# Values of a windowed attention: one projection and a trip through DRAM in place of four products on repeated tokens

## The chip, the cores and the metric

The kernel runs on one core of a Trainium2 chip. The core has TensorE (PE: matrix products into PSUM, with PEld for its weight loads), VectorE (DVE), ScalarE (ACT), GpSimd (POOL) and SyncE (SP), which here only issues DMAs. Each engine works through its own queue in order. PSUM has eight banks of 128 partitions by 512 float32. The metric is the device time of one execution in microseconds (us), median of the runs; smaller is better.

## The reference

Two transformer blocks with adaptive layernorm over x of 4 batches x 1024 tokens x 128 features, all float32. Block 0 is a linear attention and a mixture of 16 experts. Block 1 is a windowed attention with 16 heads of 8 features, then a feed-forward part that itself holds two local-attention layers ("block 1's second attention"). The change touches block 1's first attention alone:

```
h = layernorm(x) * (1 + ca) + sa
q, k, v = split(h @ w_qkv.T), 16 heads of 8
scores: causal, the last 64 tokens (key position >= 16), and the first 16 tokens as a global prefix
out = softmax(scores) @ v, heads joined, @ w_out.T
x = x + ga * out
```

## The kernel before

Activations lie with the features on the partitions and the tokens along the free dimension: `hT[b]` is 128 features x 1024 tokens of batch b. Block 1's first attention goes through 32 tiles of 128 tokens: four batches `b`, eight tiles `t` each. A tile has four chunks `c` of 32 tokens, and the 16 heads are handled as four groups of four.

For the sum of probabilities times values, 32 keys of a chunk and the four heads of a group share the 128 partitions of one product: partition 32h + k is key k for head h of the group. So V is needed in a form in which each partition block h holds the same 32 tokens, with everything but the features of head h set to zero. That is the tile `vb`, 128 x (16 x 32), where the 16 are four chunks times four groups. The mask `hm32` (a part of the constant `hx`) is one where the feature belongs to the partition block's head.

`values(b, t)` (L648 to L656) makes it. GpSimd copies the tile's tokens four times side by side into `hr` (L650). For each chunk TensorE multiplies the repeated tokens with the value weights (L653), four products of 128x128x128 into one PSUM bank `vp`, so that the repetition appears on the output's partitions. VectorE multiplies the bank with the mask into `vb` (L655).

The other functions of a step, with the lines that the prediction names:

- `maxima` (transposes of `nm`, L296) and `scores` (L267, L273, L282, row maxima on VectorE L285, then `nm` L289 and L290) work ahead: the maxima of the next tile, the scores of the one after that.
- `weights` (L666, L671, L677) forms the transposed scores for two groups at a time in PSUM, and ScalarE takes the exponentials into `pt` (L680).
- `outputs` of the tile before (L706, L715) sums probabilities times `vb` and, beside it, the denominators, in one PSUM bank `o`; VectorE then takes the reciprocal (L725) and the product `os` (L726). It reads the `vb` of its own tile and, for its first two chunks, of the tile before.
- `prefix` (L692, L693) puts the scores of the 16 prefix tokens into the second half of that same bank `o`, and ScalarE takes their exponentials `pg` (L697).
- At certain tiles: `queries` (L224), `keys` (L236, copied by VectorE L238, then masked by GpSimd into `kg` and `kx`, L240 and L243), `prefix_values` (`vgp` L255), `project_out` (`y`, L731), the layernorms (`tokens`, `normed`, with three GpSimd operations L148 to L150), and `rotary`, ten GpSimd operations that prepare tables for the second attention.

The order of a step is this (L755 and on):

```
when(g + 1, maxima); when(g + 2, scores)
queries, tokens, normed at certain tiles
when(g, weights, (0, 1)); when(g - 1, outputs)
prefix_values at t == 1
when(g, weights, (2, 3)); when(g, values); when(g, prefix)
rotary, project_out, keys at certain tiles
```

TensorE's order is exactly the order in which the code issues its work. The other engines' queues and the DMA queue are ordered by a planner, which simulates the program and issues what is ready, earlier code first; a dependency or a full set of buffers becomes a wait in the queue. `rotary` is pinned behind whatever GpSimd instruction stands before it in the code. PSUM's eight banks go to the tags "s" (4), "t" (2), "o" (1) and "m" (1); the bank "m" is shared by `vp`, `vgp`, `qp`, `kp`, `y` and the layernorm transposes. `hr` has three buffers, `vb` four. Transfers in this stage are few: before it SP issues the weights of the second attention and the table `tab` (L597 to L646), and in it two pairs of `hs` transfers (L612, L615).

Of the kernel before, what the change touches and what calls it, by code (L numbers as in the profile page):

```python
# [19 lines left out]
F32 = mybir.dt.float32  # L20
BF16 = mybir.dt.bfloat16
AF = mybir.ActivationFunctionType
ALU = mybir.AluOpType
# [3 lines left out]
P = 128  # L27
B, N, D = 4, 1024, 128
# [20 lines left out]
def adaln_blocks(ctx: ExitStack, tc: tile.TileContext, a: dict, out: bass.AP):  # L49
    nc = tc.nc  # L50
    pe, act, dve, pool = nc.tensor, nc.scalar, nc.vector, nc.gpsimd
# [4 lines left out]
    def const(name, shape, dtype=F32):  # L56
        return cp.tile(shape, dtype, tag=name, name=name)
# [54 lines left out]
    with tc.tile_pool(name="modps", bufs=2, space=PSUM) as mp:  # L112
        sc = const("sc", [P, 2, B])
        act.activation(sc, cT, AF.Silu)
        for blk in range(2):
            ps = mp.tile([P, 6, B], F32, tag="mod", name=f"modps{blk}")
            for j in range(6):
                pe.matmul(ps[:, j, :], lhsT=wmod[:, blk, j * D : (j + 1) * D], rhs=sc[:, blk, :], start=True, stop=True)
            m = const(f"mod{blk}", [P, 6, B])
# [39 lines left out]
    m = mods[0]  # L159
    hT = [hp.tile([P, N], F32, tag=f"hT{b}", name=f"hT{b}") for b in range(B)]  # L160
# [18 lines left out]
    wqkv1 = const("wqkv1", [P, 3, D])  # L179
# [24 lines left out]
    KB = 32  # L204
# [3 lines left out]
    hm32, hm64 = hx[:, 0:32], hx[:, 32:96]  # L208
    ps = both.enter_context(tc.tile_pool(name="ps", bufs=1, space=PSUM))
    kept1 = {}  # L210
# [8 lines left out]
    def queries(b, k):  # L219
        s = slice(k * BLK, (k + 1) * BLK)  # L220
        if k == 0:
            kept1[b, "q"] = of(b).tile([P, N], F32, tag="q", name=f"q1_{b}")
        qp = ps.tile([P, BLK], F32, tag="m", name=f"qp_{b}_{k}")
        pe.matmul(qp, lhsT=wqkv1[:, 0, :], rhs=hT[b][:, s], start=True, stop=True)  # L224
        act.activation(kept1[b, "q"][:, s], qp, AF.Copy, scale=scale1)

    def keys(b, k):
        s = slice(k * BLK, (k + 1) * BLK)
        if k == 0:
            kept1[b, "kx"] = of(b).tile([P, NC, 4, KB], F32, tag="kx", name=f"kx_{b}")  # L230
            kept1[b, "kg"] = of(b).tile([P, H0, PREFIX], F32, tag="kg", name=f"kg_{b}")
            kept1[b, "nmt"] = of(b).tile([P, N + 2 * KB], BF16, tag="nmt", name=f"nmt_{b}")
            pool.memset(kept1[b, "nmt"][:, N:], 0.0)
        kx, kg = kept1[b, "kx"], kept1[b, "kg"]
        kp = ps.tile([P, BLK], F32, tag="m", name=f"kp_{b}_{k}")
        pe.matmul(kp, lhsT=wqkv1[:, 1, :], rhs=hT[b][:, s], start=True, stop=True)  # L236
        kt = pre.tile([P, BLK], F32, tag="k", name=f"k1_{b}_{k}", bufs=2)
        dve.tensor_copy(kt, kp)  # L238
        if k == 0:
            pool.tensor_tensor(kg, kt[:, 0:PREFIX].unsqueeze(1).to_broadcast([P, H0, PREFIX]), bc(hm16, [P, H0, PREFIX]), ALU.mult)  # L240
        for i in range(4):
            c0 = 16 * k + 4 * i
            pool.tensor_tensor(  # L243
                kx[:, c0 : c0 + 4],
                kt[:, i * P : (i + 1) * P].rearrange("p (c k) -> p c k", k=KB).unsqueeze(2).to_broadcast([P, 4, 4, KB]),
                hm4.unsqueeze(1).unsqueeze(3).to_broadcast([P, 4, 4, KB]),
                ALU.mult,
            )

    def prefix_values(b):  # L250

        hr = pre.tile([P, 8, PREFIX], F32, tag="hrg", name=f"hrg_{b}", bufs=2)
        pool.tensor_copy(hr, hT[b][:, 0:PREFIX].unsqueeze(1).to_broadcast([P, 8, PREFIX]))
        vp = ps.tile([P, D], F32, tag="m", name=f"vgp_{b}")
        pe.matmul(vp, lhsT=hr.rearrange("p h k -> p (h k)"), rhs=wqkv1[:, 2, :], start=True, stop=True)  # L255
        vg = pre.tile([P, 2, 64], F32, tag="vg", name=f"vg_{b}", bufs=2)
        dve.tensor_tensor(vg, vp.rearrange("p (g c) -> p g c", g=2), hm64.unsqueeze(1).to_broadcast([P, 2, 64]), ALU.mult)
        kept1[b, "vg"] = vg
# [360 lines left out]
    def rotary(tab, ab, l):  # L619

        here = tc.keep_in_program_order
        qk0 = R_QK + l * 2 * DH
        for w in range(2):
            for half in range(2):
                to, of = slice(32 * half, 32 * half + 32), qk0 + w * DH + 32 - 32 * half
                here(pool.tensor_tensor(
                    ab[:, 1, :, w, to], tab[:, 1, :, w, to], rows[:, of : of + 32].unsqueeze(1).to_broadcast([P, NT, 32]), ALU.mult
                ))
            of = qk0 + w * DH
            here(pool.tensor_tensor(  # L630
                ab[:, 0, :, w, :], tab[:, 0, :, w, :], rows[:, of : of + DH].unsqueeze(1).to_broadcast([P, NT, DH]), ALU.mult
            ))
        for i in range(2):
            here(pool.tensor_scalar(ab[:, i, :, 0, :], ab[:, i, :, 0, :], 8.0, None, ALU.mult))


    m = mods[1]
    with (
        tc.tile_pool(name="w6o", bufs=1) as wo6,
        tc.tile_pool(name="w6b", bufs=2) as wb,  # L640
        tc.tile_pool(name="w6", bufs=3) as wp,
        tc.manual_schedule(engines={mybir.EngineType.PE}),
# [3 lines left out]
        nc.sync.dma_start(out=tab, in_=a["tab"])  # L646
        def values(b, t):

            hr = wp.tile([P, 4, 4, KB], F32, tag="hr", name=f"hr_{b}_{t}")
            pool.tensor_copy(hr, hT[b][:, t * P : (t + 1) * P].rearrange("p (c k) -> p c k", k=KB).unsqueeze(2).to_broadcast([P, 4, 4, KB]))  # L650
            vp = ps.tile([P, 4, D], F32, tag="m", name=f"vp_{b}_{t}")
            for c in range(4):
                pe.matmul(vp[:, c, :], lhsT=hr[:, c].rearrange("p h k -> p (h k)"), rhs=wqkv1[:, 2, :], start=True, stop=True)  # L653
            v = wp.tile([P, 16, 32], F32, tag="vb", name=f"vb_{b}_{t}", bufs=4)
            dve.tensor_tensor(v, vp.rearrange("p c (j e) -> p (c j) e", e=32), hm32.unsqueeze(1).to_broadcast([P, 16, 32]), ALU.mult)  # L655
            kept1[b, t, "v"] = v  # L656

        def weights(b, t, js):
            nt = f"{b}_{t}"
# [68 lines left out]
        def project_out(b, k):  # L728
            s = slice(k * BLK, (k + 1) * BLK)
            yp = ps.tile([P, BLK], F32, tag="m", name=f"y1_{b}_{k}")  # L730
            pe.matmul(yp, lhsT=wout1, rhs=kept1[b, k, "os"], start=True, stop=True)  # L731
            dve.scalar_tensor_tensor(xT[b][:, s], yp, mods[1][:, 2, b : b + 1], xT[b][:, s], ALU.mult, ALU.add)  # L732
# [18 lines left out]
        def when(g, f, *args):  # L751
            if 0 <= g < NG8:
                f(*divmod(g, NT), *args)

        for g in range(NG8 + 2):  # L755
            b, t = divmod(g, NT)
            ahead = b + 1 < B
            when(g + 1, maxima)
            when(g + 2, scores)
            if ahead and t in (2, 4):  # L760
                queries(b + 1, t // 2 - 1)
            for after, k, f in ((6, 0, tokens), (8, 0, normed), (11, 1, tokens), (13, 1, normed)):
                if (g - after) % NT == 0 and 0 <= (g - after) // NT < B - 1:
                    f((g - after) // NT, k, "h3")
            for at, k, f in ((1, 0, tokens), (3, 0, normed), (5, 1, tokens), (7, 1, normed)):
                if g == at:
                    f(B - 1, k, "h2")
            when(g, weights, (0, 1))
            when(g - 1, outputs)
            if ahead and t == 1:  # L770
                prefix_values(b + 1)
            when(g, weights, (2, 3))
            when(g, values)
            when(g, prefix)
            if t == 5 and 0 < b <= DEPTH:
                rotary(tab, abs_[b - 1], b - 1)
            if g % 4 == 1 and g > 4:
                project_out((g - 5) // NT, (g - 5) % NT // 4)
            if ahead and t in (3, 5):
                keys(b + 1, t // 2 - 1)  # L780
# [6 lines left out]
    with (  # L787
# [214 lines left out]
        for l in range(DEPTH):  # L1002
            for b in range(B):
                g = (l * B + b) * NT
# [18 lines left out]
        for g in range(-2, tiles + 12):  # L1023
            side = steps.get(g, [])
            when(g, scores)
            when(g + 2, project, 0)
            when(g - 1, flip, 0)
            when(g + 2, project, 1)
            when(g - 1, flip, 1)
            when(g + 1, turn, 0)  # L1030
            when(g - 2, outputs, 0)
            for f, args in side[:1]:
                f(*args)
            when(g + 1, turn, 1)
            when(g - 2, outputs, 1)
            when(g, values)
            when(g - 3, back)

            f0 = g - 7 if g < tiles - 2 else g - 6
            if f0 % 4 == 0 and 0 <= f0 < tiles and g != tiles - 1:  # L1040
                project_out(f0 // (B * NT), f0 // NT % B, f0 % NT // 4)
            for f, args in side[1:]:
                f(*args)
# [148 lines left out]
```

## Time and profile before

| | |
|---|---|
| median of 3 runs | 1399.29 us (1398.83 to 1407.56) |
| profiled execution | 1399.1 us, span of its instructions 1397.3 us |
| the stage of the change, first `vp` matmul to last `os` | 342.6 to 654.3 us |
| mean granted TensorE clock | 0.982 of full speed |
| `vp` matmuls L653 | 256 records (two for each product), from 342.6 to 649.1 us |
| `hr` copies L650 on GpSimd | 32, 0.61 us each |
| masking multiplies L655 on VectorE | 32, 0.69 us each |

A row of the timeline is start, duration, engine, line, operation, output and inputs with partitions x elements, and how often. In groups of instructions the numbers are total busy time, mean time of one in ns, and the idle time before them with what ended it. The chain of waits is followed back from the last instruction, at each step to what released it; its rows are start, time on the chain, engine, tile, line. "PEclk" or "granted clock" is the TensorE clock as a share of full speed.

### The profile page before, as it was taken

The page shows a single profiled execution, that of the slowest core. Times are in us where ns is not written, and L with a number is a line of the kernel's source. Part 1 is how long each engine was busy: PE and PEld are TensorE (multiplying, and loading weights), DVE is VectorE, ACT ScalarE, POOL GpSimd, SP SyncE. Part 2 cuts the span into 40 slices and gives each one's busy share as a digit, 9 for nine tenths or more (in the row PEclk, how much of TensorE's full clock was granted, in tenths as well). Part 3 has the DMA queues.
Part 4 walks back from the last instruction along what each step waited for, and adds up shares of the span by engine and source line. Part 5 has one row for each costly group of instructions (what it writes and reads, how often), then busy time and mean ns, then how long its engine had stood idle before and what let it go on. Part 6 is the DMA issues. An engine that isn't in the chain of part 4 may idle for free.

```text
span 1397.3 us, 33849 instructions
## 1 busy us (share of the span) xinstructions
PE 1311.6 (94%) x13908; PEld 810.3 (58%) x13908; DVE 885.1 (63%) x2090; ACT 702.8 (50%) x1453; POOL 730.6 (52%) x750
## 2 busy tenths in 40 slices
PE   5799988997999999998899999999999999999997
PEld 4544544444777677676466566656666566666553
DVE  5655444523555555554788778877788777887753
ACT  2463532321222222222576776767667776677752
POOL 4454537461232405211987676666767667766620
PEclk9799999998999999999899999999999999999999
DMA  6031221213000000000111111111211111111111
GB/s 180 0 123 55 68 67 57 69 53 121 3 3 3 17 3 18 3 3 3 24 33 45 38 43 32 24 43 33 48 34 25 43 32 43 44 35 36 40 35 30
DMA packets 38655, 56.14 MB, mean 40 GB/s; under 512 B 6331, under 2 KB 18661, under 8 KB 38373
## 3 DMA queue, kind: packets, MB, share of 16 engines
q1 hardware_dynamic: 37204, 52.44, 14.1%
q8 instruction: 110, 1.80, 0.5%
q10 hardware_dynamic: 1296, 1.54, 0.3%
q14 instruction: 45, 0.36, 0.1%
HBM read 27.24 MB, written 2.36 MB: 21 GB/s over the span
## 4 chain that ended last, share of the span: by engine, by line
PE 77%; DVE 8%; POOL 7%; ACT 3%; issue 3%; DMA 1%; POOLq 0%; ACTq 0%; SPq 0%
PE qk L802 7%; PE v L844 4%; PE o L903 4%; PE s L873 4%; PE t L677 4%; PE yp L927 4%; PE qktr L829 4%; PE ptr L890 3%; PE o L715 3%; PE gm L961 3%; PE h L494 3%; PE a L970 3%; PE ym L978 3%; PE vp L653 3%; POOL u L498 2%
## 5 line engine op out<-in xcount | busy, mean ns | idle before, releaser
L819 POOL TENSOR_TENSOR co<-co,si 128x512 f32<-128x512 f32 x128 | 162.7, 1273 | 129.1 <-DVE si L812 128.7
L818 POOL TENSOR_TENSOR ss<-ss,nhalf 128x16 f32<-128x16 f32 x64 | 187.2, 2925 | 4.7
L882 ACT ACTIVATE pr<-s,mx,ss 128x128 f32<-128x128 f32 x512 | 186.5, 480 | 1.8
L805 ACT ACTIVATE sq<-qk 128x512 f32<-128x512 f32 x128 | 79.5, 621 | 171.7 <-PE qk L802 98.1
L802 PE MATMUL qk<-wqkv,hs 128*128 128x512 f32 x256 | 137.2, 620 | 0.8 <-DVE xT L732 0.8
L498 POOL TENSOR_TENSOR u<-u,cw 128x512 f32<-128x512 f32 x64 | 81.1, 1270 | 93.2 <-ACT u L497 74.5
L494 PE MATMUL h<-hT,w 128*128 128x512 f32 x256 | 122.1, 597 | 1.6 <-DVE g L500 1.6
L877 DVE TENSOR_REDUCE mx<-s 128x4 f32<-128x512 f32 x128 | 82.3, 684 | 56.1 <-PE s L873 56.0
L500 DVE TENSOR_TENSOR g<-u,h 128x512 f32<-128x512 f32 x64 | 43.7, 685 | 114.8 <-POOL u L498 112.6
L285 DVE TENSOR_REDUCE mx<-s 128x4 f32<-128x448 f32 x128 | 70.9, 616 | 70.4 <-PE s L282 70.4
L680 ACT ACTIVATE pt<-t 128x384 f32<-128x384 f32 x128 | 55.8, 488 | 116.9 <-PE t L677 116.9
L650 POOL COPY hr<-hT 128x512 f32<-128x512 f32 x32 | 19.5, 614 | 176.4 <-PE vp L653 172.3
L807 DVE TENSOR_TENSOR co<-qk,ab 128x512 f32<-128x512 f32 x128 | 87.7, 685 | 28.6 <-ACT sq L805 28.3
L890 PEld LDWEIGHTS ptr<-ident,pr 128*128 128x128 f32 x512 | 63.6, 141 | 64.8 <-issue 53.4
L829 PE MATMUL qktr<-ident,co 128*128 128x128 f32 x512 | 78.1, 275 | 11.5 <-POOL co L821 10.5
L497 ACT ACTIVATE u<-h 128x512 f32<-128x512 f32 x64 | 38.3, 598 | 97.3 <-PE h L494 90.4
L903 PE MATMUL o<-vs,pt 128*64 128x65 f32 x1024 | 86.9, 228 | 0.0
L812 DVE TENSOR_TENSOR si<-qk,ab 128x512 f32<-128x512 f32 x128 | 86.8, 678 | 0.0
L903 PE MATMUL o<-ve,pt 128*64 128x65 f32 x1024 | 86.6, 227 | 0.0
L814 DVE TENSOR_REDUCE ss<-sq 128x8 f32<-128x512 f32 x128 | 86.2, 673 | 0.0
L494 PEld LDWEIGHTS h<-hT,w 128*128 128x128 f32 x256 | 47.8, 192 | 61.9 <-issue 53.5
L903 PEld LDWEIGHTS o<-ve,pt 128*64 128x64 f32 x1024 | 69.2, 137 | 23.1 <-issue 16.1
(234 smaller groups left out, 3060.6 us busy)
## 6 DMA issues: line engine op xcount, KB each, us to landing
cw<-cd SPq DMA_DIRECT2D x128, 128.0 KB, 3.1
ve<-vs SPq DMA_DIRECT2D x120, 130.0 KB, 2.3
hs_m<-hT SPq DMA_DIRECT2D x24, 128.0 KB, 2.2
xin<-in_x SPq DMA_DIRECT2D x4, 512.0 KB, 6.9
hs<-hT SPq DMA_DIRECT2D x8, 256.0 KB, 2.9
out<-out SPq DMA_DIRECT2D x8, 256.0 KB, 2.5
hs<-hT SPq DMA_DIRECT2D x8, 255.8 KB, 3.7
w<-in_w SPq DMA_DIRECT2D x3, 512.0 KB, 5.0
```

Of the source, the lines that this page charges most:

```text
L494: pe.matmul(h, lhsT=w[:, c * P : (c + 1) * P], rhs=hT[b][:, blk(k)], start=True, stop=True)
L498: pool.tensor_tensor(u, u, kept[b, k, "cw"][:, c, :], ALU.mult)
L802: pe.matmul(ps, lhsT=hs[l, b][:, t * P : (t + 1) * P], rhs=wl[l][0][:, w, :], start=True, stop=True)
L807: dve.tensor_tensor(co, ph, abs_[l][:, 0, t, w, :].unsqueeze(1).to_broadcast([P, HEADS, DH]), ALU.mult)
L812: dve.tensor_tensor(si.rearrange("p h (i e) -> p h i e", i=2), ex, sn, ALU.mult)
L814: dve.tensor_reduce(ss[:, w, :], sq, AX.X, ALU.add)
L818: pool.tensor_tensor(ss, ss, nhalf[:, 0:2].unsqueeze(2).to_broadcast([P, 2, HEADS]), ALU.pow)
L819: pool.tensor_tensor(co, co, si, ALU.add)
L829: pe.transpose(tp[:, i, :], co[:, i * P : (i + 1) * P], ident)
L882: act.activation(pr[:, c, :], S[j][:, c, :], AF.Exp, bias=mx[:, j, c : c + 1], scale=rq[:, j, c : c + 1])
L890: pe.transpose(tp[:, c, :], pr[:, c, :], ident)
L903: pe.matmul(o[qs, c, :], lhsT=pt[:, c, qs], rhs=vv[:, 2 * c + j, :], start=True, stop=True)
```

## The change

V of a tile is projected once: one product of the tile's 128 tokens with the value weights, tokens on the partitions. ScalarE copies it from PSUM to `v` in SBUF. A DMA writes `v` to a DRAM tile `vd` (64 KB), and four DMAs read it back, one for each partition block h, each placing token k of chunk c at partition 32h + k: 32 partitions x 4 chunks x 128 features, 64 KB in pieces of 512 bytes. GpSimd multiplies the result `vr` with the mask into `vb`. All five DMAs are issued by SP. `hr` and the VectorE multiply are gone. `vb` has five buffers instead of four.

The values of a tile are made one step sooner: `values(0, 0)` stands before the loop, and step g makes the values of tile g + 1 at the place where it made those of tile g.

```diff
         tc.tile_pool(name="w6o", bufs=1) as wo6,
+        tc.tile_pool(name="w6d", bufs=3, space=bass.MemoryType.DRAM) as dr6,
...
         def values(b, t):
 
-            hr = wp.tile([P, 4, 4, KB], F32, tag="hr", name=f"hr_{b}_{t}")
-            pool.tensor_copy(hr, hT[b][:, t * P : (t + 1) * P].rearrange("p (c k) -> p c k", k=KB).unsqueeze(2).to_broadcast([P, 4, 4, KB]))
-            vp = ps.tile([P, 4, D], F32, tag="m", name=f"vp_{b}_{t}")
-            for c in range(4):
-                pe.matmul(vp[:, c, :], lhsT=hr[:, c].rearrange("p h k -> p (h k)"), rhs=wqkv1[:, 2, :], start=True, stop=True)
-            v = wp.tile([P, 16, 32], F32, tag="vb", name=f"vb_{b}_{t}", bufs=4)
-            dve.tensor_tensor(v, vp.rearrange("p c (j e) -> p (c j) e", e=32), hm32.unsqueeze(1).to_broadcast([P, 16, 32]), ALU.mult)
-            kept1[b, t, "v"] = v
+            vp = ps.tile([P, D], F32, tag="m", name=f"vp_{b}_{t}")
+            pe.matmul(vp, lhsT=hT[b][:, t * P : (t + 1) * P], rhs=wqkv1[:, 2, :], start=True, stop=True)
+            v = wp.tile([P, D], F32, tag="v", name=f"v_{b}_{t}", bufs=2)
+            act.copy(v, vp)
+            vd = dr6.tile([P, D], F32, tag="vd", name=f"vd_{b}_{t}")
+            nc.sync.dma_start(out=vd, in_=v)
+            vr = wp.tile([P, 4, D], F32, tag="vr", name=f"vr_{b}_{t}")
+            for h in range(4):
+                nc.sync.dma_start(out=vr[32 * h : 32 * h + 32], in_=vd.rearrange("(c k) f -> k c f", k=KB))
+            vb = wp.tile([P, 16, 32], F32, tag="vb", name=f"vb_{b}_{t}", bufs=5)
+            pool.tensor_tensor(vb, vr.rearrange("p c (j e) -> p (c j) e", e=32), hm32.unsqueeze(1).to_broadcast([P, 16, 32]), ALU.mult)
+            kept1[b, t, "v"] = vb
...
+        values(0, 0)
         for g in range(NG8 + 2):
...
             when(g, weights, (2, 3))
-            when(g, values)
+            when(g + 1, values)
             when(g, prefix)
```

## The prediction

> **What bounds the kernel now.** I read the page's busy times first, then the busy times of stretches inside the stage that the change touches (block 1's first attention, 342 to 653 us), then the chain of waits through it.
>
> ```profile
> PE 1311.6 (94%) x13908; PEld 810.3 (58%) x13908; DVE 885.1 (63%) x2090; ACT 702.8 (50%) x1453; POOL 730.6 (52%) x750
> ```
>
> The average does not decide; the stretches do (columns: length, then busy us of each engine, granted clock, DMA share, GB/s):
>
> ```profile
> core 0: us, PE busy (x) PEld busy (x) DVE busy (x) ACT busy (x) POOL busy (x), PEclk, DMA share, GB/s
> 420.00:500.00 80.00, 79.16 (x1608) 57.26 (x1592) 44.34 (x95) 22.53 (x54) 27.18 (x33) 1.00 0.04 9
> 580.00:653.00 73.00, 72.36 (x1625) 55.26 (x1622) 34.34 (x71) 20.81 (x51) 5.66 (x8) 1.00 0.01 3
> ```
>
> TensorE is busy 99% of the stage at full granted clock; VectorE 55%, GpSimd 34%, ScalarE 28%, the DMA engines near nothing. A busy TensorE need not be at its peak, so I checked in the chain of waits that the values' matmuls lie on the path:
>
> ```profile
> 433.20 0.42 PE vgp L255 x2
> ...
> 434.04 0.86 PE t L677 x16
> 434.91 1.09 PE vp L653 x8
> 436.00 0.22 PE o L692 x2
> ```
>
> From 345 to 653 the chain is TensorE alone; `vp` L653 holds 11.0% of those 308 us, 1.06 us a tile. The row above it is the twin of what the change leaves: `vgp`, one 128x128 float32 product (two records, x2), takes 0.42 us where four take 1.09.
>
> **What the change removes from the path.** A tile goes from four products to one: 1.09 - 0.42 = 0.67 us. The timeline agrees: `vp`'s eight records start 445.73, the next matmul at 446.73, 1.00 us, and six records of eight at the even pace of 0.11 us are 0.67.
> - Steps 1 to 30: 30 x 0.67 = 20.1 us.
> - Step 0: its `vp` ran at a granted clock of 0.67 (336 to 346 us) and took 1.87 us to the next matmul (342.63 to 344.50); six eighths are 1.4, I take 1.3.
> - Step 31 has no values any more: 0.9.
> - Tile 0's product now stands before the loop, behind the scores that end at 330.26. TensorE idles there from 330.3 to 333.0 for VectorE's `nm` (2.77 us): cost 0; without that gap, 0.4.
>
> Together -22.3 us.
>
> **What it adds, off the path if it is in time.** VectorE loses 32 x 0.69 us, GpSimd 32 `hr` copies of 0.61. ScalarE gains 32 copies 128x128 (its `nmt` copies of that size: 0.26). GpSimd gains 32 multiplies 128x512; its nearest rows are 1.04 us (`kx` L243) and 1.28 (L630), I take 1.28 because that row too reads two float32 tiles of SBUF. GpSimd goes from 27 to 33 us in 80: not a bound. SP gains 160 issues, nearest rows 0.31 to 0.60 us each, 2.7 us a tile and 2 us of waiting for the write in a step of 9 us; only four `hs` transfers share its queue there.
>
> The question is whether V arrives before its reader. The DMA rows, the nearest there are (KB each, median us from issue to landing):
>
> ```profile
> cw<-cd SPq DMA_DIRECT2D x128, 128.0 KB, 3.1
> ...
> out<-out SPq DMA_DIRECT2D x8, 256.0 KB, 2.5
> ...
> cd<-ct SPq DMA_DIRECT2D x8, 32.0 KB, 1.9
> ```
>
> `ct` to `cd` to `cw` is the same pattern through DRAM: the read's issue follows the write's landing by under 0.1 us (issue 127.49, landed 129.04, next issue 129.09). From the start of a tile's `vp`: ScalarE is in two exponentials until +1.03 (`vp` at 434.84, they end 435.87), its copy ends +1.30, SP issues +1.36, the write lands +3.3 (1.9; bounds 1.5 to 2.6 by `cd`), the fourth read is issued +5.1 (three issues of about 0.6 before it), lands +8.2 (3.1; bounds 2.2 by `ve`, 3.4 by `cw`'s slow ones), the multiply ends at about **+9.5 us** (bounds 8.0 to 10.7).
>
> The reader is `outputs`, now two steps on. Today a tile's `vp` starts and the next tile's first `o<-pt,vb` follows after 17.8 us typically (445.73 to 463.52), 14.9 at least through step 28 (624.00 to 638.88). The two steps shrink by 1.34, and the first two chunks read the tile before (+0.37, 442.94 to 443.31): **13.9 to 16.8 us** against 9.5. Hidden, with 4.4 us spare. At the end the steps are short: for tile 31, 641.67 to 651.40 is 9.73, less 0.67 and 0.89, plus 0.37: 8.5. It is late by 1.0 us (bounds 0 to 2.2). Tile 30 has 10.9: in time.
> Tile 0: SP's weight loads were issued until 333.7 and `tab` landed by 341; behind it, write 342.5, reads 346.5, multiply 348; its reader comes at 351.2 - 1.3 = 349.9. In time by 2 us; if each transfer needs the 5 to 7 us of that burst, up to 4 us once.
>
> **What is late next.** `prefix` (L692) writes the PSUM bank that VectorE's `os` (L726) reads, and follows `vp`. In tile 11:
>
> ```profile
> 455.31 1.16 PE L653 MATMUL vp<-wqkv,hr 128*128 128x128 f32 x8
> ...
> 455.97 0.29 DVE L726 TENSOR_TENSOR os<-o,rs 128x128 f32<-128x128 f32 x1
> ...
> 456.31 0.49 PE L692 MATMUL o<-q,kg 128*128 128x128 f32 x2
> ```
>
> L726 ends at 456.26, L692 starts 0.05 later: here the 0.67 us comes back. The same distance in the other tiles is mostly 0.80 to 0.86 (0.15 left after the change), 0.05 in tiles 11 and 19, 0.25 in 14 and 22, 0.52 in 6. If the bank is waited for, with a lag of 0.05 us: 2 x 0.67 + 2 x 0.47 + 0.2 + 0.1 = 2.6 us; if not, 0. I take 2.6, because a lag of 0.05 is also what TensorE's transposes show behind `nm` (332.97 to 333.02).
> `vp`'s bank, tag "m" with one buffer, is freed by ScalarE's copy at +1.30 instead of VectorE's multiply (434.84 to 436.72 today): sooner, if the copy goes ahead of the `pg` exponential.
>
> **A rule against the change.** VectorE's small `nm` subtraction takes 0.22 us alone and 1.00 beside a GpSimd multiply:
>
> ```profile
> 442.55 0.22 DVE L290 TENSOR_TENSOR nm<-mx,nm 128x64 bf16<-128x64 f32 x1
> ...
> 463.17 1.00 DVE L290 TENSOR_TENSOR nm<-mx,nm 128x64 bf16<-128x64 f32 x1
> ```
>
> [...]
> It is not on the path by the trace: from `nm`'s end to the transposes that read it there are 3.7 us or more in every steady step, 3.0 after the change, against a worst stretch of 1.3. Cost 0.
>
> **Sum.** -22.3 + 2.6 + 1.0 = -18.7 us on the profiled execution's 1399.1 (span 1397.3, 1.8 around it), 0.2 under the median of 1399.29: **1380**. Its own range, bounds of the unknowns taken in, is 1375 to 1385.
>
> **Rivals.**
> 1. *GpSimd's or ScalarE's queue eats the spare time.* Each takes instructions in the planner's order. A V that has landed may stand behind `kx` (4 x 1.04) and a layernorm (2.6): 6.6 - 4.4 = 2.2 us, six times; behind `rotary`, which is pinned after the multiply of its step and takes 8.8 us, 4.4 twice: at most 22 us. And if the copy of V goes behind `pg`, the next users of bank "m" (eight `y1`, six `kp`) wait some 0.6 us, 8 in all. For it: GpSimd waited on TensorE for `hr` 172 us, so it does stall in order. Against: the spare time exceeds any single group but `rotary`. Half of the worst, 11 us: about 1391, range 1385 to 1402.
> 2. *The round trip is slow: slower than before.* If each of the two serial transfers takes the 7.3 us that `tab` took in the burst, V needs 9.5 + 5.4 + 4.2 = 19 us against 13.9 to 16.8, up to 5 too late, and since each stall also lengthens the next window about half of a mean 4 is paid per tile: 31 x 2 = 62 us, 1399.1 - 22.3 + 62 = 1439. It loses once a stall exceeds 0.67 us a tile, that is from a chain of some 17 us. Against: the stage moves 2 to 9 GB/s, and `cd`, `ve` and `out` land in 1.9 to 2.5 us.
> 3. *The matmuls removed were not what the stage waits for*, so their time comes back as idle: 1395 to 1400. Against: the unbroken TensorE chain.
>
> **How the numbers follow.** Forecast 0.60, rival 1 0.22, rival 2 0.11, rival 3 0.07. A measurement here tells about 1%, 14 us, from no change: faster by over 1% means under 1385.3, the forecast. Rival 1 is within 1% but for a tail that joins rival 2. Faster 0.60, same 0.27, slower 0.13. The range holds forecast and rivals 1 and 3 up to 1400, low end 1374 (no bank wait, no late tile, rounding of the first step): 0.85.
>
> **What would show it.** Right: `vp` with 64 records; steps of about 9.0 us instead of 9.6; TensorE still 98% busy; `hr` gone; the stage 18 to 20 us shorter and block 2 unchanged. Tile 31's first `o<-pt,vb` behind GpSimd's multiply; L692 behind `os` in tiles 11, 14, 19, 22. Wrong: TensorE waiting for `vb` in steady steps, named after GpSimd (rival 1 where V had landed, rival 2 where it had not), or for ScalarE's copy.

## The result, and the profile after

The changed kernel takes 1402.63 us in the median (1397.22 to 1408.6), the kernel before 1400.07 us in runs taken beside it; the ratio is 1.0007, 95% interval 0.9991 to 1.0023. **No change**, where 1380 was forecast; 1402.63 lies above the range of 1374 to 1400. Executions of both kernels differ among themselves by up to 11 us with the mean granted clock (for most of the kernel before, in the runs beside the experiments, 1397.21 to 1400.55 us at 0.982 or 0.983 and 1406.45 to 1408.33 us at 0.976 or 0.977), so I rely on medians and, inside a profile, on stages.

The profiled execution took 1402.61 us, span 1400.8. The page's busy times and, from its slices of the span, TensorE and the clock granted to it:

```profile
PE 1310.1 (94%) x13716; PEld 799.5 (57%) x13716; DVE 872.4 (62%) x2058; ACT 708.2 (51%) x1485; POOL 751.5 (54%) x750
...
PE   5799988998999999998799999999999999999997
...
PEclk9799999998999999798999999999999999999999
```

TensorE has 192 records fewer, as intended (`vp` has 64), and yet 1310.1 busy us against 1311.6. Fewer matmuls take almost the same time: some of them ran at a lower clock. The stretches shown in the prediction had clock 1.00 and TensorE busy for 79.16 us of 80 and 72.36 of 73. After (length, busy us of each engine, clock, DMA share, GB/s):

```profile
core 0: us, PE busy (x) PEld busy (x) DVE busy (x) ACT busy (x) POOL busy (x), PEclk, DMA share, GB/s
420.00:500.00 80.00, 77.23 (x1553) 53.31 (x1548) 38.91 (x84) 22.70 (x61) 32.60 (x33) 0.94 0.15 41
580.00:653.00 73.00, 69.96 (x1530) 52.33 (x1502) 30.60 (x63) 21.45 (x56) 12.84 (x11) 0.92 0.12 34
```

Two things are new: TensorE idles for 2.8 and 3.0 us in these stretches (0.8 and 0.6 before), and the clock is no longer full. What TensorE waited for between 345 and 655 us (engine, tile and line, what released it: us in total, times, longest):

```profile
PE o L697 <- DVE os L731: 6.9, 8, 1.6
PE kp L236 <- DVE xT L737: 2.5, 3, 0.8
PE o L720 <- POOL vb L660: 1.4, 1, 1.4
PE o L711 <- ACT pg L702: 0.5, 1, 0.5
```

L697 is `prefix` (L692 before). The rows for `kp` and `pg` are those of the kernel before; the first and the third are new. V itself comes late once, in tile 31, by 1.4 us. Now one of the eight waits from both sides, in tile 14. The stretch that ends with the wait, the wait, what follows, and what follows that:

```profile
470.00:480.40 10.40, 9.55 (x189) 5.99 (x189) 5.44 (x11) 3.14 (x8) 5.11 (x5) 1.00 0.12 35
480.40:483.80 3.40, 1.81 (x27) 1.46 (x23) 3.14 (x10) 1.03 (x3) 3.40 (x5) 1.00 0.04 11
483.80:494.10 10.30, 10.30 (x135) 6.64 (x139) 3.64 (x6) 1.41 (x4) 8.91 (x9) 0.50 0.11 30
494.10:500.00 5.90, 5.90 (x124) 4.07 (x117) 1.52 (x3) 1.57 (x5) 0.15 (x1) 1.00 0.08 21
```

TensorE idles 1.59 us, and then runs for 10.3 us at half clock (granted clock 0.50): 135 matmul records where the 10.4 us before the wait had 189. The same 16 products L682 take 1.80 us to the next matmul at half clock (from 583.28) and 0.96 us at full clock (from 594.36). Half of the time at half clock counted as lost, an estimate from these two figures, that costs three times the wait.

In the stage (from the end of block 0's last `y` matmul, L508, to the end of the last `y1` matmul, L736; L731 before) half clock lasts 51.0 us after and 10.2 before. By the same estimate the 40.8 us more cost half of that, some 20 us. Half clock follows the waits at 403.0, 482.1, 563.7 and 575.0 (30.7 us together, in stretches of 3.41, 10.24, 3.41 and 13.65) and that of tile 31 at 650.8 (6.7 us inside the stage); the remaining 3.4 us lie at the stage's start. The wait of 0.90 us at 616.7 us is followed by none. The stage took 329.46 us and takes 331.56.

Why `os` is late shows VectorE's timeline in the same tile (start, duration, engine, line, operation, output and inputs):

```profile
479.50 1.16 DVE L290 TENSOR_TENSOR nm<-mx,nm 128x64 bf16<-128x64 f32 x1
480.58 0.47 DVE L141 BATCH_NORM_STATS2 st_h<-xt_h 128x6 f32<-128x128 f32 x2
480.97 0.35 DVE L143 BATCH_NORM_AGGREGATE mv_h<-st_h 128x2 f32<-128x6 f32 x4
481.43 1.05 DVE L146 TENSOR_TENSOR xh_h<-xt_h,mv_h 128x512 f32<-128x512 f32 x1
482.40 0.95 DVE L730 RECIPROCAL rs<-o 128x128 f32<-128x128 f32 x1
483.38 0.29 DVE L731 TENSOR_TENSOR os<-o,rs 128x128 f32<-128x128 f32 x1
```

GpSimd and TensorE beside it:

```profile
475.29 4.03 POOL L243 TENSOR_TENSOR kx<-k,hm 128x512 f32<-128x512 f32 x4 [5.75 <-DVE k L238]
479.28 1.29 POOL L660 TENSOR_TENSOR vb<-vr,hx 128x512 f32<-128x512 f32 x1
...
481.90 1.71 POOL L630 TENSOR_TENSOR ab<-tab,rows 128x512 f32<-128x512 f32 x1
...
481.65 0.49 PE L651 MATMUL vp<-wqkv,hT 128*128 128x128 f32 x2
...
483.73 0.69 PE L697 MATMUL o<-q,kg 128*128 128x128 f32 x2 [1.59 <-DVE os L731]
```

And the kernel before in the same tile, where L692 followed `os` without a wait:

```profile
486.13 0.20 DVE L290 TENSOR_TENSOR nm<-mx,nm 128x64 bf16<-128x64 f32 x1
...
487.11 0.71 DVE L146 TENSOR_TENSOR xh_h<-xt_h,mv_h 128x512 f32<-128x512 f32 x1
...
488.72 0.29 DVE L726 TENSOR_TENSOR os<-o,rs 128x128 f32<-128x128 f32 x1
...
489.27 0.39 PE L692 MATMUL o<-q,kg 128*128 128x128 f32 x2
```

The small subtraction `nm` takes 0.96 us longer while GpSimd's new multiply L660 runs, the layernorm's subtraction L146 0.34 longer beside `rotary` L630. The multiply stands where it does because GpSimd works in order too: the last read of its tile had landed 3.4 us before it started, and `keys`' four products `kx` were ahead of it. VectorE works in order: the matmuls L720 of `outputs` end at 480.43, and the reciprocal, which reads what they wrote, starts at 482.40, behind L146. So the reciprocal and `os`, which touch no tile of GpSimd's, are 1.3 us late; TensorE arrives 0.67 us sooner. Of the waits of 0.9 us and more at L697, four stand in steps that hold a layernorm (403, 482, 564, 617), the fifth in the step after one (575), where `rotary` has pushed the layernorm's GpSimd part and the multiply onto VectorE's next `nm` (1.22 us). In four of these five steps the multiply started 3.4 to 4.2 us after its data had landed, behind `kx` (three times) or behind `rotary` and the layernorm; only at 617 it followed the landing at once.

**Theory.** The matmuls' time did go. It came back through a chain: GpSimd's multiply, now placed by the transfer's landing and by what GpSimd has ahead of it, holds VectorE; `os` stands behind; TensorE waits at L697; most of the longer waits are followed by half clock. **Rivals**: the transfers themselves or their traffic; GpSimd's multiply wherever it stands; TensorE's reach for the bank, which any other order would mend; and half clock that has nothing to do with the waits.

### The profile page after: what moved, and what is told of

It reads as the page before. It is cut to its first block, busy times and chain, and to the rows that moved or that the text cites. A ratio compares the mean times of both kernels' runs of the same rounds, so it can differ in the third digit from the quotient of the medians.

```text
span 1400.8 us, 33706 instructions
## 1 busy us (share of the span) xinstructions
PE 1310.1 (94%) x13716; PEld 799.5 (57%) x13716; DVE 872.4 (62%) x2058; ACT 708.2 (51%) x1485; POOL 751.5 (54%) x750
## 4 chain that ended last, share of the span: by engine, by line
PE 70%; DVE 10%; POOL 7%; issue 3%; ACT 3%; DMA 1%; SPq 0%; POOLq 0%; ACTq 0%; DVEq 0%
PE qk L808 7%; PE v L850 4%; PE o L909 4%; PE s L879 4%; PE yp L933 4%; PE qktr L835 4%; PE ptr L896 3%; PE t L682 3%; PE gm L967 3%; PE h L494 3%; PE a L976 3%; PE ym L984 3%; PE o L720 3%; POOL u L498 2%; PE s L273 2%
## 5 line engine op out<-in xcount | busy, mean ns | idle before, releaser
L808 PE MATMUL qk<-wqkv,hs 128*128 128x512 f32 x256 | 140.2, 633 | 0.8 <-DVE xT L737 0.8
L660 POOL TENSOR_TENSOR vb<-vr,hx 128x512 f32<-128x512 f32 x32 | 41.3, 1292 | 177.2 <-DMA vr<-vd 168.8
```

The costliest lines, as they stand in the source:

```text
L808: pe.matmul(ps, lhsT=hs[l, b][:, t * P : (t + 1) * P], rhs=wl[l][0][:, w, :], start=True, stop=True)
```

## The experiments

Each ratio is to the kernel before, run on the same chip, with its 95% interval. Stage lengths are from the one profiled execution of each.

**1. The transfers alone.** The kernel before, with the write and the four reads added; nothing uses what they bring.

```diff
             kept1[b, t, "v"] = v
+            vd = dr6.tile([P, D], F32, tag="vd", name=f"vd_{b}_{t}")
+            nc.sync.dma_start(out=vd, in_=v.rearrange("p j e -> p (j e)")[:, 0:D])
+            vr = wp.tile([P, 4, D], F32, tag="vr", name=f"vr_{b}_{t}", bufs=1)
+            for h in range(4):
+                nc.sync.dma_start(out=vr[32 * h : 32 * h + 32], in_=vd.rearrange("(c k) f -> k c f", k=KB))
```

> The kernel before, which in addition writes 64 KB of each tile's vb to DRAM and reads them back with four DMAs into a tile that nobody uses. Theory A: the transfers cost nothing, 1397 to 1401 us, TensorE clock in 420 to 580 us 1.00. Theory B (traffic slows the stage): 1410 to 1421 us, since the change gave back some 22 us.

1407.04 us (1398.56 to 1408.25), ratio 1.0029 [1.0002, 1.0057]; the median lies above the 1397 to 1401 us expected. The profiled execution is the shortest of the ten, 1398.56 us; its stage took 329.46, to the hundredth that of the kernel before, with the traffic there:

```profile
420.00:500.00 80.00, 79.16 (x1620) 57.15 (x1616) 44.35 (x95) 22.52 (x54) 27.15 (x33) 1.00 0.15 42
```

42 GB/s instead of 9, and TensorE is neither idle nor slowed. The median's upper bound, 0.57% or 8 us, is less than half of the 20 us that are missing, and the profile shows nothing of it. The transfers by themselves are not the cause.

**2. `prefix` one step later**, so that it no longer meets `os`: in the changed kernel, and as a control in the kernel before (there `when(g, values)` stays).

```diff
             when(g + 2, scores)
+            when(g - 1, prefix)
...
             when(g + 1, values)
-            when(g, prefix)
```

> The changed kernel with prefix moved from behind the values to the next step, behind the scores, so that TensorE does not come to the shared PSUM bank until VectorE's os has long been written. Theory A (VectorE's in-order queue, held up by GpSimd's masking multiply, writes os late; prefix L697 waits 6.9 us in sum, and after such waits the TensorE clock is 0.5 for 3.4 to 13.7 us at a time, some 18 us): the L697 waits on os vanish, the clock in 420 to 580 us is 1.00, the time is 1376 to 1383 us. Theory B (the DMA traffic or the masking slows the stage in another way): TensorE still waits or runs slow elsewhere, 1395 us or more.

> The kernel before with the same move of prefix and nothing else. Theory A: there prefix never waited for os and the clock was 1.00, so nothing is to be had: 1397 to 1401 us. If the move itself brings time (another reason), below 1390 us, and the run with both does not tell the cause.

Changed kernel: 1401.72 us (1400.64 to 1403.93), 0.9998 [0.9975, 1.0021]. Control: 1409.93 us (1408.4 to 1418.13), 1.0071 [1.0043, 1.0099]. Both expectations missed, since the move has a price of its own: the waits at L697 are gone from the steady steps, others took their place. The changed kernel's waits:

```profile
PE y L736 <- ACT v L653: 4.9, 7, 0.7
PE s L267 <- ACT nmt L297: 4.6, 19, 0.2
PE kp L236 <- DVE xT L737: 2.5, 3, 0.8
PE kp L236 <- ACT v L653: 2.1, 3, 0.7
```

With `prefix` out of the way, `y1` and `kp` follow `values` directly and wait for the bank "m". Compared with its control the change is worth 8.2 us in the medians and 8.4 in the stage (331.48 against 339.92). It has 30.7 us at half clock there (20.5 of them from 332.8 on, behind no wait at L697), 17.0 more than the control, and TensorE idles 3.0 us more; without these, by the estimate above 8.4 + 8.5 + 3.0 = 19.9 us, near the 22.3 us of the removed products. The clock from 420 to 580 us is 1.00 under these many waits, none longer than `kp`'s 0.84 us. It did fall at 397.6 us for 3.41 us, behind a wait of 0.70 us and during `kp`'s; the same pair of waits at 478 and 558 us brought no fall.

**3. The mask on ScalarE**, in the changed kernel: GpSimd's multiply becomes four activations with a scale per partition.

```diff
-            pool.tensor_tensor(vb, vr.rearrange("p c (j e) -> p (c j) e", e=32), hm32.unsqueeze(1).to_broadcast([P, 16, 32]), ALU.mult)
+            ve = vr.rearrange("p c (j e) -> p (c j) e", e=32)
+            for h in range(4):
+                act.activation(vb[:, :, 8 * h : 8 * h + 8], ve[:, :, 8 * h : 8 * h + 8], AF.Identity, scale=hm32[:, 8 * h : 8 * h + 1])
```

> The changed kernel with the masking multiply on ScalarE (four products of 128x128 by a mask column) in place of GpSimd's one. [...] If VectorE's delay has another cause than GpSimd: waits as before the edit, 1397 to 1405 us.

1391.13 us (1384.78 to 1397.84), 0.9916 [0.9878, 0.9953]: faster by 0.8%, and within the 1382 to 1392 us expected if GpSimd's multiply holds VectorE up. In the same tile VectorE has its old durations, and L697 (now L699) waits 0.31 us:

```profile
478.40 0.20 DVE L290 TENSOR_TENSOR nm<-mx,nm 128x64 bf16<-128x64 f32 x1
...
479.38 0.71 DVE L146 TENSOR_TENSOR xh_h<-xt_h,mv_h 128x512 f32<-128x512 f32 x1
...
481.35 0.49 PE L699 MATMUL o<-q,kg 128*128 128x128 f32 x2 [0.31 <-DVE os L733]
```

All waits there together are 0.8 us in three, the stage is 313.90 us, and the clock from 420 to 635 us 1.00. This run doesn't say which GpSimd instruction had done it: without the multiply `rotary`, pinned behind it, runs earlier too. And the clock did fall once, at 363.7 us, behind a wait of only 0.35 us.

**4. GpSimd's multiply alone**, in the kernel before: `vb` multiplied by the mask once more, the result unused.

```diff
             kept1[b, t, "v"] = v
+            vz = wp.tile([P, 16, 32], F32, tag="vz", name=f"vz_{b}_{t}", bufs=1)
+            pool.tensor_tensor(vz, v, hm32.unsqueeze(1).to_broadcast([P, 16, 32]), ALU.mult)
```

> The kernel before, in which GpSimd also multiplies each tile's vb by the mask into a tile that nobody uses: GpSimd's part of the change without the transfers and with all four products. [...] If GpSimd's multiply does not hold VectorE up: 1399 us and no wait at L692.

1400.05 us (1399.18 to 1408.69), 1.0009 [0.9986, 1.0033]. I had expected it to cause waits at `prefix`, and it caused none:

```profile
420.00:500.00 80.00, 79.16 (x1621) 57.12 (x1619) 44.85 (x95) 21.99 (x52) 36.89 (x40) 1.00 0.04 9
```

GpSimd works 36.9 us instead of 27, more than in the changed kernel, and nothing comes of it. The `nm` subtractions sum to 9.0 us over the stage against 9.4 in the kernel before and 15.5 in the changed one. This multiply cannot start before VectorE's own multiply of the same tile has ended, and `nm` and `os` stand ahead of that one on VectorE. So a multiply of this size does not do harm in every place. In the changed kernel it can start when the last read has landed, 6.2 us after `vp` in the median, and starts after 7.2 us in the median, from tile 2 on up to 10.2 us where GpSimd has other work ahead; in these steps that meets `nm`.

**5. The layernorm behind `os`.** If the harm lies in what stands ahead of the reciprocal on VectorE, it is enough to move that. `tokens`, which issues the layernorm's statistics and L146, goes behind `outputs`: in the changed kernel, in the kernel before as a control, and with the ScalarE mask as well.

```diff
-            for after, k, f in ((6, 0, tokens), (8, 0, normed), (11, 1, tokens), (13, 1, normed)):
+            for after, k, f in ((8, 0, normed), (13, 1, normed)):
...
-            for at, k, f in ((1, 0, tokens), (3, 0, normed), (5, 1, tokens), (7, 1, normed)):
+            for at, k, f in ((3, 0, normed), (7, 1, normed)):
...
             when(g - 1, outputs)
+            for after, k, f in ((6, 0, tokens), (11, 1, tokens)):
+                if (g - after) % NT == 0 and 0 <= (g - after) // NT < B - 1:
+                    f((g - after) // NT, k, "h3")
+            for at, k, f in ((1, 0, tokens), (5, 1, tokens)):
+                if g == at:
+                    f(B - 1, k, "h2")
```

> The changed kernel with the layernorm's tokens called behind outputs instead of ahead of the weights, so that VectorE has the reciprocal and os ahead of the layernorm's work; GpSimd's multiply and the DMAs stay. Theory A: os comes in time in the layernorm tiles, the waits at L697 of 0.9 to 1.6 us vanish, the clock in 420 to 580 us is near 1.00, 1378 to 1388 us. If GpSimd's multiply or the DMAs cost something of their own beside the delay of os: 1392 us or more.

> The kernel before with the layernorm's tokens behind outputs and nothing else. Theory A: there os was in time, so the move brings nothing: 1396 to 1401 us where the kernel before has 1399, and the 19 us of the run with both belong to the change. If the move itself brings the time: 1380 to 1390 us.

> Both edits together: the mask on ScalarE and the layernorm's tokens behind outputs. Theory A: no wait at prefix is left in steady steps, 1376 to 1385 us and the least spread between runs. If the two edits remove the same delay: no better than the better of the two.

- Changed kernel with the move: **1379.75 us** (1377.42 to 1390.21), 0.985 [0.980, 0.990], the fastest of all.
- Kernel before with the move (on another chip than the other two): 1399.81 us (1398.26 to 1408.04), 1.0006 [0.9981, 1.003]. The move alone brings nothing.
- With the mask on ScalarE too: 1385.68 us (1380.74 to 1391.55), 0.989 [0.9836, 0.9945]; no better than the move alone.

The first one's waits and stretches:

```profile
PE kp L236 <- DVE xT L737: 2.5, 3, 0.8
PE y L736 <- DVE os L731: 1.4, 1, 1.4
PE o L720 <- POOL vb L660: 1.1, 1, 1.1
```

```profile
420.00:500.00 80.00, 79.16 (x1697) 55.39 (x1699) 44.84 (x93) 25.24 (x67) 32.39 (x33) 1.00 0.16 45
```

At L697 one wait of 0.2 us is left; TensorE is as busy as in the kernel before, at full clock, and gets through 1697 records where it had 1608. The stage is 307.31 us, 22.15 shorter than before. GpSimd holds VectorE no less than in the changed kernel: the `nm` subtractions sum to 19.2 us, up to 1.35 each. They only no longer stand, with a layernorm between, ahead of an `os` that TensorE is about to need. So the chain goes through VectorE's order, and the block by GpSimd costs little by itself.

The move does a second thing: it puts the layernorm's four transposes on TensorE between `outputs` and `prefix`. In tile 14's step:

```profile
474.87 0.66 PE L743 MATMUL in_h<-ident,xT 128*128 128x128 f32 x4
...
476.75 0.29 DVE L731 TENSOR_TENSOR os<-o,rs 128x128 f32<-128x128 f32 x1
...
477.10 0.49 PE L697 MATMUL o<-q,kg 128*128 128x128 f32 x2
```

Counted from the end of the matmuls of `outputs`, `os` ends after 2.11 us where it was 3.25, and TensorE is ready for L697 after 2.30 us where it was 1.71. By an estimate from these four figures, VectorE's order took 1.14 us of the 1.59 us wait away and TensorE's later arrival the last 0.45, in this step and in tile 22's. No run separates the two; a wait of 0.45 us is as long as those that bring no half clock in experiment 7.

**6. Only the layernorms for `h3` moved**, those of `h2` at steps 1 and 5 left in their old place.

> The changed kernel with only the three batches' h3 tokens behind outputs; the h2 tokens of the first steps stay where they were, so the wait of 0.68 us for the shared bank at 350 us does not arise. Theory A: as with all tokens moved or a little better, 1375 to 1382 us, no wait at L697 over 0.5 us between 390 and 620 us.

1387.09 us (1378.64 to 1393.06), 0.9887 [0.9848, 0.9926], above the 1375 to 1382 expected. One wait over 0.2 us is left at L697, in step 5, and half clock follows it for 10.2 us:

```profile
395.31 0.72 PE L697 MATMUL o<-q,kg 128*128 128x128 f32 x2 [0.92 <-DVE os L731]
```

```profile
395.40:405.60 10.20, 9.36 (x55) 3.47 (x57) 1.44 (x2) 0.65 (x2) 3.67 (x4) 0.50 0.12 34
```

`kp`'s usual wait of 0.84 us is no candidate for this fall: it begins at 399.2 us, when the clock has been at half for 3.8 us. From 420 to 580 us the clock is full again.

**7. The price of a wait.** The kernel before, its VectorE delayed in four steps (t == 4) by two or by four copies 128x512 from PSUM that nothing uses (the diff shows four). There is no transfer, no change of GpSimd, no matmul less.

```diff
-            dve.reciprocal(rs, O[:, 1, :])
+            if t == 4:
+                for i in range(4):
+                    dl = wp.tile([P, 4, P], F32, tag="dl", name=f"dl_{b}_{t}_{i}", bufs=1)
+                    dve.tensor_copy(dl, O[:, 1:2, :].to_broadcast([P, 4, P]))
+                tc.keep_in_program_order(dve.reciprocal(rs, O[:, 1, :]))
+            else:
+                dve.reciprocal(rs, O[:, 1, :])
```

> The kernel before, with two VectorE copies of 128x512 out of PSUM (some 0.65 us each, results unused) put ahead of the reciprocal in the tiles with t == 4, four in all: os is 1.3 us later there and prefix, which had 0.8 us to spare, waits about 0.5 us. Theory A: waits this short leave the clock at 1.00; 4 x 0.5 = 2 us, 1400 to 1402 us against 1399. If any wait of TensorE lowers the clock: 1405 us or more.

> The same with four copies: os 2.6 us later, prefix waits about 1.8 us, four times. Theory A: each such wait is followed by 3.4 to 13.7 us at a granted clock of 0.5, so the price is the wait (7 us) and half of the slow time (7 to 27 us) again: 1413 to 1433 us. If a wait costs only itself: 1405 to 1408 us.

Two copies: four waits at L692 of 0.36 to 0.47 us, no half clock behind them, 1402.95 us (1400 to 1402 expected), 1.0014 [0.9984, 1.0044]. Four copies: four waits of 2.2 to 2.3 us, 9.0 in all, and 1422.63 us, 1.0156 [1.011, 1.0201]; the stage is 23.9 us longer. The first of the four waits, and then the stretch that ends with it, the one behind it, and the next:

```profile
396.88 0.49 PE L692 MATMUL o<-q,kg 128*128 128x128 f32 x2 [2.33 <-DVE os L732]
```

```profile
388.00:397.20 9.20, 6.87 (x166) 5.88 (x162) 8.48 (x22) 2.33 (x5) 3.35 (x4) 1.00 0.02 4
397.20:407.40 10.20, 9.36 (x57) 3.48 (x56) 1.63 (x3) 0.65 (x2) 3.15 (x4) 0.50 0.00 0
407.40:417.00 9.60, 9.60 (x209) 7.22 (x209) 6.02 (x19) 2.87 (x7) 4.08 (x5) 1.00 0.01 3
```

All four waits are followed by half clock, for 10.24, 6.83, 6.83 and 10.24 us. 9.0 us of waiting and, by the same estimate, half of 34 us are 26; the stage shows 23.9. Here nothing but VectorE's copies and so the waits was put in, with no transfer and no work of GpSimd's, so waits do bring the half clock, and it costs more than they do.

**8. V two tiles ahead**, `tokens` behind `prefix_values`, to take tile 31's wait away as well.

```diff
         values(0, 0)
+        values(0, 1)
...
-            when(g + 1, values)
+            when(g + 2, values)
```

(The layernorm's calls move as in experiment 5, but behind `prefix_values`; `vb` has six buffers and `vr` two.)

> The changed kernel with the layernorm's tokens behind prefix_values and the values two tiles ahead (six vb buffers, two vr). It should keep what moving the tokens alone gave (1379.75 us) and take away the wait of 1.1 us for the last tile's vb and of 0.7 us for the shared bank: 1374 to 1380 us. If the order of the planner shifts elsewhere, up to 1390.

1386.07 us (1381.73 to 1386.4), 0.989 [0.9856, 0.9923], a miss. The wait for `vb` is gone, and the new place of `tokens` makes another: its transposes use the bank "m" behind `vgp`, and half clock follows from 354.0 to 367.7.

```profile
352.36 0.66 PE L743 MATMUL in_h<-ident,xT 128*128 128x128 f32 x4 [1.55 <-DVE vg L257]
```

## Why the prediction was wrong

**"What the change removes from the path", -22.3: right.** Where the changed kernel runs at full clock its steps are 0.67 to 0.72 us shorter (8.88, 9.17 and 9.26 us where there were 9.55, 9.89 and 9.93). Experiment 5 has 22.15 us less in the stage, and 20.1 less in the medians than its control (1379.75 against 1399.81). Rival 3's condition, that the matmuls were not what the stage waits for, is refuted.

**"What it adds, off the path if it is in time": right, and on the safe side.** From the start of `vp` to the end of the multiply it took 8.5 us in the median, 9.5 predicted. The two rows (KB, median us from issue to landing) are below what I took from the neighbours, 3.1 for a read and 1.9 for the write:

```profile
vr<-vd SPq DMA_DIRECT2D x128, 64.0 KB, 2.0
...
vd<-v SPq DMA_DIRECT2D x32, 64.0 KB, 1.5
```

TensorE waited for `vb` in no steady step, in tile 31 1.4 us (predicted 1.0). Rival 2 is refuted. Of rival 1 the queue came true and the price did not: in five tiles a V that had landed stood 3.4 to 4.2 us behind other work of GpSimd, `kx` or `rotary` and the layernorm, and was still in time for its reader.

**"What is late next", 2.6 us: right place, too small.** The waits at `prefix` are there, eight of them, with 6.9 us. Tiles 11, 14, 22 and 6 had been named and waited 0.33, 1.59, 1.60 and 1.09 us; tile 19, named too, did not wait, and the waits of 0.94 and 0.90 us in tiles 23 and 27 were not foreseen. I took the distances from the trace of before and shortened them by TensorE's 0.67 us, as though `os` stayed where it was. It moved as well, the other way, by 1.3 us in tile 14.

**"A rule against the change", "Cost 0": the step that failed.** VectorE's subtractions do take longer beside GpSimd's work: L290 takes 1.16 us beside the multiply and 0.20 without it, L146 1.05 beside `rotary`'s L630 and 0.71 without it; why is not shown. The worst stretch of 1.3 us was my estimate, the length I took for the multiply. No run shows it as a bound; the longest `nm` takes 1.22 us in the changed kernel and 1.35 in experiment 5. I judged the block by `nm`'s own reader, which has 3.7 us to spare, and that was true: no wait for `nm` shows in the steady steps. What counted was who stands behind `nm` in VectorE's queue. In the layernorm steps that is L146 and then `os`, which TensorE needs within a microsecond. Experiments 3 and 5 each break this chain, at its first and at its last link, and the gain comes back, by the medians about half of it in the one and nearly all of it in the other (there with some help from TensorE's transposes).

**The term that was missing: what a wait does to the clock.** I priced a wait at its length. In this kernel one of about 0.9 us and more was mostly followed by 3.4 to 13.7 us at half clock: 6.9 us of waits at L697 became some 15 us more (half of 30.7, by the estimate above), and with the one of tile 31 and the stage's start about 20. The trace of before had the row, and I passed it by:

```profile
339.87 0.85 PE L666 MATMUL t<-cb 32*128 32x384 bf16 x2 [1.91 <-ACT pt L680]
```

```profile
340.20:347.00 6.80, 6.75 (x38) 5.55 (x38) 0.69 (x1) 1.42 (x5) 0.62 (x1) 0.50 0.01 2
```

I even used the lower clock of that stretch to size step 0's `vp`, without asking what had lowered it.

**The sum as measured**, for the stage: -22.3 for the products, +5.8 for more idle time of TensorE (17.3 us against 11.6), +20.4 for half clock (half of the 40.8 us) is +3.9; the stage shows +2.1. The same sum gives -21.1 for experiment 5 (-0.5 and 1.7; measured -22.15) and -17.2 for experiment 3 (0.3 and 4.8; measured -15.6). It closes to within 2 us, too high twice and too low once. The rest of the kernel behind the stage took 743.0 us after and 741.8 before, with no edit there.

Rival 3 did say "their time comes back", between 1395 and 1400, but as idle time; as that came only about a quarter, the rest as matmuls that take nearly twice as long (L682 above: 1.80 us and 0.96) on an engine that reads as busy.

**Not settled**: what exactly makes the clock fall. Waits of 2.2 to 2.3 us at L692 did it four times in four, those of 0.9 to 1.6 us at L697 mostly (0.90 us at 616.7 did not), `kp`'s 0.84 us never alone, and once it fell behind 0.35 us. Length alone does not decide: the 1.4 us wait ahead of the last `y1` was followed by no fall for 10 us in the kernel before. What the traces do show is when it falls. In each of the two traces, before and after, the changes of the clock in the stage lie on one grid of 3.41 us, and after the change the falls behind the waits at L697 come at the end of the grid's interval that holds the wait (waits that end at 404.07, 483.73, 565.26 and 575.94 us, falls at 405.37, 483.88, 565.80 and 576.04). The wait at 616.7 is the only one of 0.9 us and more at L697 that a boundary of the grid cuts, at 617.0, into 0.27 and 0.63 us; whether that is why no fall came is not shown.

## What to carry to other kernels

When an engine is held up, ask who stands behind it in that engine's queue, not who reads the held-up result: here VectorE's queue, worked through in order, handed a delay of 1.3 us to an `os` that has nothing to do with its cause. When a change brings TensorE sooner to a meeting point, compute both sides of that meeting again, and price a new wait in a dense stage with the low clock that may follow (here mostly 3.4 to 13.7 us at 0.50); the trace before may have a wait to take the price from, as it did here. A gain that vanishes while TensorE stays busy is looked for in the clock's row, and may come back from reordering alone: moving one call made 1380 us out of 1403.

## What the runs showed of the hardware

Short waits can lower TensorE's clock. In the traces before and after it was granted either fully (1.00) or at half (0.50), never between, and the half-clock stretches in the stage last 3.41, 6.83, 10.24 or 13.65 us, in experiment 2 also 20.48 us, multiples of 3.41. In experiment 7 four waits of 2.2 to 2.3 us in a stage where TensorE is otherwise 99% busy were followed by 34 us of half clock, four of 0.36 to 0.47 us by none, and in experiment 6 a wait of 0.92 us was followed by 10.24.

A transfer that depends on another through DRAM took little in this stage: from the issue of the 64 KB write to the landing of the fourth 64 KB read 5.0 us in the median (1.2 to 6.2 us after the start of `vp`), and in experiment 1 42 GB/s of such traffic left every engine's busy time in 80 us within 0.11 us of what it was.
